# The third layer of a position-bias MLP on tiles of 32 keys by four sums, with lane transfers given out at fixed slots

## The chip, the cores and the metric

The kernel runs on one core of one Trainium2 chip. The time of a run is the device time of that core in microseconds (us). Everything is in float32.

## The reference, cut to what matters

The program has two layers on x of shape (2, 512, 32, 32). The first is a deformable attention with 8 heads of 64 channels: each head of each image looks from 1024 queries at 64 sampled keys, and the score gets a bias from a small MLP on the distance between query and key. The second is a plain attention over 1024 tokens. The change touches only the bias MLP:

```python
pos = grid_q[:, :, None, :] - grid_kv[:, None, :, :]     # 16 (image, head) groups, 1024 queries, 64 keys, 2
bias = jnp.sign(pos) * jnp.log1p(jnp.abs(pos))
bias = jax.nn.relu(bias @ cpb_w1 + cpb_b1)               # 2 -> 128
bias = jax.nn.relu(bias @ cpb_w2 + cpb_b2)               # 128 -> 128
bias = (bias @ cpb_w3 + cpb_b3).reshape(b, GROUPS, H * W, Hd * Wd)   # 128 -> 1
sim = jnp.einsum('bhid,bhjd->bhij', qh, kh) + bias
attn = jax.nn.softmax(sim, axis=-1)
out = jnp.einsum('bhij,bhjd->bhid', attn, vh)
```

There are 16 x 1024 x 64 pairs of query and key, and each needs the 128 x 128 product of the second layer.

## The kernel before, in words

**Slots.** The first stage works through `NS` = 256 slots, 16 for each of the 16 groups. A slot holds 4 keys by 1024 queries. In each, VectorE (DVE) builds the first layer `h1` (`st_layer1`, line L681, three buffers, two slots ahead). TensorE (PE) multiplies it by the second layer's weights (`st_layer2`, L698). The 128 hidden channels go out in four quarters z of 32, and four matmuls with 32 output columns each, one per key q, stand side by side in the PE array. So one eviction tile has on its 128 partitions 4 keys by 32 channels. ScalarE (ACT) evicts the four quarters with the relu: the even ones into `rx` (L707, three buffers), the odd ones into a long-lived tile and into `ub` (L709). PSUM has three tiles for this (`zp`, bufs=3).

**Sums over channels.** The third layer has one output, so its weights (`sc`) can be applied to whole tiles, and channels can be added before PE sees them. The channels are sorted by the sign of their third-layer weight, so that in quarters 1 and 3, which are evicted with the weight as a scale, lanes that are to be added share one sign. `st_sum(s, 0)` and `st_sum(s-1, 2)` are DVE instructions (L717) that add quarter 0 to quarter 1 and quarter 2 to quarter 3. Then an accumulating DMA on GpSimd's queue (POOL, L719) adds `ub` into the slot's long-lived tile. What is left of a slot is 4 keys by 32 sums.

**Folding lanes.** DMAs then fold the lanes (partitions) of a tile further. `st_fold` adds half of the lanes onto the other half, which frees half of the tile; `st_join` copies the partner tile's lanes into the freed half (SP queue, L743) and adds the partner's other lanes on top (POOL queue). Two slots so become one tile of 8 keys by 16 sums. `st_fold2` and `st_join2` (copies at L752) do the same with two such tiles: 16 keys by 8 sums. All adds go through `add` (L736), a POOL accumulate-DMA which is held behind the one before it in program order. The long-lived tile of slot s has the name `ua` (s%4 = 0, four buffers), `uc` (s%4 = 2, two) or `uo` (odd s, three). The tile `uc` becomes free when `st_join2` has read it.

**Third layer.** `st_layer3` (L784) multiplies such tiles by block weights (`w3f`) into the group's score tile in PSUM. For each 8 slots it issues one set of four matmuls with 32 columns each (two tiles by two halves of the queries), 12 slots after the first of the 8 slots. The product of queries and keys (L767) goes into the same PSUM tile. The last four slots of the last group aren't folded but multiplied tile by tile (`w3u`).

**Order.** The loop at the end of the stage writes out each slot by hand: the DVE sum of the slot before, the fold and join steps that are due, the next table load (`load_tables`, L650, a broadcast DMA `fb` on SP), `st_layer1(s+2)`, `st_layer2(s)`, tables, `st_sum(s, 0)`, then a step of background work (`later`, which makes the sampled keys and values of the next groups: `chain` and `sample`, with DMA loads `xn`, `xnt`, `wk` on SP), a step of the softmax of an earlier group (`softmax_steps`), and `st_layer3`. `st_join` follows its first slot by 3 slots, `st_fold2` by 4, `st_join2` by 6. Engines run their own instructions in this order; a DMA that waits holds up what is behind it on the queue of its engine.

After the stage come projection (`project`, L988), MLP (L1041, L160) and the second layer (L1200, L1276, L1298), which use the same product routines before and after the change.

Of the kernel before, what the change touches and what calls it, by code (L numbers as in the profile page):

```python
# [14 lines left out]
P = 128  # L15
# [42 lines left out]
def conv_seq_kernel(ctx: ExitStack, tc: tile.TileContext, x, xt, kst, pst, cst, vec, wsm, outw, w1, w2, wl, wlt, brow, out):  # L58
# [25 lines left out]
    w3f = cp.tile([P, 48], F32, name="w3f")  # L84
# [122 lines left out]
    with tc.tile_pool(name="lp", bufs=2) as lp:  # L207
# [11 lines left out]
        prod = ph.tile([P, 12, 2, 8, 8], F32, name="prod")  # L219
# [22 lines left out]
        nc.gpsimd.dma_start(out=pz[:, 0:413], in_=pst)  # L242
        nc.gpsimd.dma_start(out=ident, in_=kst)

        def load(b, k, wq=None):
# [21 lines left out]
        w2t, crow, tri, eight, chan, mask = (  # L267
            pz[:, a:b] for a, b in ((0, 128), (128, 256), (256, 384), (384, 392), (392, 393), (393, 413))
        )
        wb = vs[:, VOFF["w3"] : VOFF["w3"] + 2]  # L270
        po_, rn, t8, pc, dc, k8, one = (
            pw_[:, a:b] for a, b in ((0, 1), (1, 3), (3, 4), (4, 5), (5, 6), (8, 16), (128, 256))
# [15 lines left out]
        def order():  # L288
            nc.vector.tensor_scalar(k8, eight, rn[:, 1:2], 8.0, ALU.is_le, ALU.mult)
            nc.vector.tensor_reduce(t8, k8, AX.X, ALU.add)  # L290
            free, bound = ([t.rearrange("p (a b l) -> p b a l", a=2, b=2)[:, i] for t in (place, crow)] for i in (0, 1))
            nc.vector.tensor_scalar(bound[0], bound[1], t8, 64.0, ALU.is_ge, ALU.mult)
            nc.vector.tensor_tensor(bound[0], bound[0], bound[1], ALU.add)
            nc.vector.tensor_scalar(free[0], free[1], t8, None, ALU.add)
            nc.vector.tensor_scalar(perm, place, pc, None, ALU.is_equal)

        def arrange():
            nc.gpsimd.memset(prod, 0.0)
            ps = simp.tile([P, 512], F32, name="sim")
            nc.tensor.matmul(ps[:, 0:P], w2t, perm, start=True, stop=True)  # L300
            for z in range(4):
                for u in range(4):
                    nc.tensor.matmul(
                        ps[32 * u : 32 * u + 32, P + 2 * z : P + 2 * z + 2], perm[:, 32 * z : 32 * z + 32], wb,
                        start=True, stop=True,
                    )
            nc.scalar.copy(cw2, ps[:, 0:P])
            nc.scalar.copy(
                sc[:, 0:8].rearrange("p (a z) -> p z a", a=2), ps[:, P : P + 8].rearrange("p (z a) -> p z a", a=2)
            )  # L310
            nc.gpsimd.tensor_scalar(sc[:, 8:9], sc[:, 1:2], 0.0, 2.0, ALU.is_ge, ALU.mult)
            nc.gpsimd.tensor_scalar(sc[:, 8:9], sc[:, 8:9], 1.0, None, ALU.subtract)
            nc.gpsimd.tensor_scalar(sc[:, 0:4], sc[:, 0:4], sc[:, 8:9], None, ALU.mult)
            for z in (1, 3):
                nc.gpsimd.tensor_tensor(sc[:, 4 + z : 5 + z], sc[:, 4 + z : 5 + z], sc[:, z : z + 1], ALU.mult)
            nc.gpsimd.tensor_scalar(w3f[:, 16:32], mask[:, 0:16], sc[:, 8:9], None, ALU.mult)
            nc.gpsimd.tensor_scalar(w3u[:, 28:32], mask[:, 16:20], sc[:, 8:9], None, ALU.mult)
# [4 lines left out]
        def chain(ci):  # L322
# [52 lines left out]
            else:  # L375


                for m in range(3):
# [71 lines left out]
            fe = ph.tile([P, 5, n], F32, tag="fe", name="fe")  # L450
            pos, ab, u, ln, er = (fe[0:64, i, :] for i in range(5))
            nc.vector.tensor_scalar(pos, thf[0:64, 2 * n : 3 * n], -1.0, gq[0:64], ALU.mult, ALU.add)
# [8 lines left out]
            nc.vector.scalar_tensor_tensor(er, u, 1.0, ab, ALU.subtract, ALU.subtract)  # L461
            rc = acc.rearrange("p a k y x -> p (a k y x)")[0:64, 0:n]
            nc.vector.reciprocal(rc, u)
            nc.vector.tensor_tensor(er, er, rc, ALU.mult)
            nc.vector.tensor_scalar(pos, pos, 0.0, 2.0, ALU.is_ge, ALU.mult)
            yield
            nc.vector.tensor_tensor(ln, ln, er, ALU.subtract)
# [10 lines left out]
        def sample(ci):  # L478
# [10 lines left out]
            sg = ph.tile([P, 5, 2, K * J], F32, tag="fe", name="sg")  # L489
            hat = sg[:, 0:4].rearrange("p a f j -> p (a f j)")[:, 0 : 4 * K * J]  # L490
# [4 lines left out]
            nc.vector.tensor_tensor(sg[:, 4], sg[:, 0], sg[:, 1], ALU.mult)  # L495
            hx = ph.tile([P, 2, K, J], F32, tag="hx", name="hx")
# [5 lines left out]
            for i, (b, k) in enumerate(G):  # L502
                g = b * NCH + k
                xnt = ph.tile([P, 8, P], F32, name="xnt")
# [12 lines left out]
                kv, uv = (ph.tile([P, J], F32, name=name) for name in ("kv", "uv"))  # L517
                rowwise, natural = "p (e i t) -> p e i t", "p (i e t) -> p e i t"
                for f in range(2):
                    r, v = slice(64 * f, 64 * f + 64), sg[:, 4, f, i * J : (i + 1) * J]  # L520
                    nc.scalar.activation(
                        uv[r].rearrange(rowwise, e=2, t=16), v[r].rearrange(natural, e=2, t=16), AF.Copy,
                        scale=col("bn1b", k)[r],
                    )
# [6 lines left out]
                for t in range(8):  # L531
# [5 lines left out]
                nc.scalar.activation(  # L537
                    kv.rearrange(rowwise, e=2, t=16), ps[:, 0:J].rearrange(natural, e=2, t=16), AF.Copy,
                    scale=bns[:, k : k + 1],
                )  # L540
# [150 lines left out]
        def st_layer2(s):  # L691
            h1 = h1s.pop(s)
            r = []
            for z in range(4):
                ps = zp.tile([P, 2, 512], F32, name="ps2")
                for h in range(2):
                    for q in range(4):
                        nc.tensor.matmul(  # L698
                            ps[32 * q : 32 * q + 32, h, :], cw2[:, 32 * z : 32 * z + 32],
                            h1[:, 16 * h : 16 * h + 16, q, :], start=True, stop=True,  # L700
                        )
                name, bufs = (
                    ("rx", 3), (("ua", 4), ("uo", 3), ("uc", 2), ("uo", 3))[s % 4], ("rx", 3), ("ub", 3)
                )[z]
                o = lp.tile([P, 2, 512], F32, name=name, bufs=bufs)
                if z % 2 == 0:
                    nc.scalar.activation(o, ps, AF.Relu, bias=sc[:, 4 + z : 5 + z])  # L707
                else:
                    nc.scalar.activation(o, ps, AF.Relu, bias=sc[:, 4 + z : 5 + z], scale=sc[:, z : z + 1])  # L709
                r.append(o)  # L710
                if z % 2 == 1:
                    evicted.setdefault(s, []).append(nc.cur_bb.bb.instructions[-1])
# [28 lines left out]

        def st_join(s):
            nc.sync.dma_start(out=lanes(s, 1), in_=lanes(s + 1, 1))  # L743
# [6 lines left out]
        def st_join2(s):  # L750
            for o, i in zip(twos(s, 1), twos(s + 2, 1)):
                nc.sync.dma_start(out=o, in_=i)  # L752
            for o, i in zip(twos(s, 1), twos(s + 2, 0)):
                add(o, i)


        def st_layer3(s):
            gi, i = divmod(s // 8, NSL // 8)
            b, k, f = groups[gi]
            if gi not in sims:  # L760
                sims[gi] = simp.tile([P, 512], F32, name="sim")
            if f == 0 and i == 1:

                assert state[chain_of[b, k][0]] is None
                sims[gi + 1] = simp.tile([P, 512], F32, name="sim")
                for f_, h_, o, h in QUADS:
                    nc.tensor.matmul(  # L767
                        sims[gi + o][h_, :], kz[f_, b * NCH + k, :], qa[f_, b, k, h * 512 : (h + 1) * 512],
                        start=(o == 1), stop=False,
                    )  # L770
            w = w3f[:, 16 - 16 * i : 48 - 16 * i]
            parts = [[(w, sums[s + 4 * e][1])] for e in range(2)]
            if s + 8 == NS:

                w = [w3u[:, 28 - 16 * i - 4 * o : 60 - 16 * i - 4 * o] for o in range(4)]
                parts[1] = [(w[o], sums[s + 4 + o][1]) for o in range(4)]
                parts[1].append((w[3], sums[s + 7][3]))
                parts[0] = 4 * [None] + parts[0]
            for m in range(len(parts[1])):
                for h in range(2):  # L780
                    for e in range(2):
                        if parts[e][m]:
                            q, (w_, t) = 64 * h + 32 * e, parts[e][m]
                            nc.tensor.matmul(  # L784
                                sims[gi][q : q + 32, :], w_, t[:, h, :], start=(i == 0 and f == 0),
                                stop=(i == 1 and m == len(parts[e]) - 1),
                            )
            for o in range(8):
# [58 lines left out]
        for s in range(NS):  # L847
            if s > 0:
                st_sum(s - 1, 2)
            if s % 2 == 0 and 2 <= s < NS - 2:  # L850
                st_fold(s - 2)
            if s % 2 == 1 and 3 <= s < NS - 1:
                st_join(s - 3)
            if s % 4 == 0 and s >= 4:
                st_fold2(s - 4)
            if s % 4 == 2 and s >= 6:
                st_join2(s - 6)
# [15 lines left out]
            if bg is not None and state.get(len(CHAINS) - 1, 0) is None:  # L873
# [8 lines left out]
                opt = op.tile([P, 2, 512], F32, name="opt")  # L882
# [12 lines left out]
            if s % 8 == 4 and s >= 12:  # L895
                st_layer3(s - 12)
                if s % NSL == 4:
                    tails.append(softmax_steps(s // NSL - 1))
        st_sum(NS - 1, 2)
        st_layer3(NS - 8)  # L900
# [35 lines left out]
    with ExitStack() as top, tc.tile_pool(name="wp", bufs=1) as wp:  # L936
# [199 lines left out]
        project(0, op0[0], op0[1], opt, lambda: [next(tail, None) for _ in range(3)])  # L1136
# [313 lines left out]
def _order(np):  # L1450
# [4 lines left out]
    place = np.where(z % 2 == 1, 8 * (l // 4) + l % 4 + 4 * (z // 2), 32 * (z // 2) + l)  # L1455
    crow = np.broadcast_to(place, (P, P))
    tri = d[:, None] < d[None, :]
    eight = np.broadcast_to(8 * np.arange(1, 9), (P, 8))
    four = (4 * (d % 4) + d // 32)[:, None] == np.arange(16)
    alone = (d // 32)[:, None] == np.arange(4)  # L1460
    return np.concatenate([crow, tri, eight, d[:, None], four, alone], axis=1).astype(np.float32)
# [88 lines left out]
```

## Time and profile before

| what | value |
|---|---|
| three runs | 2617.99, 2619.43, 2620.34 us |
| profiled execution, its own time | 2621.32 us |
| its span | 2619.2 us |
| mean granted TensorE clock | 1.00 |
| PE busy in the span | 2603.2 us, 99% |
| DVE | 2313.1 us, 88% |
| ACT | 1750.3 us, 67% |
| POOL | 815.7 us, 31% |
| DMA packets' time on queue q0 (issued by POOL) | 54.6% of 16 engines |
| DMA packets' time on queue q1 (issued by SP) | 15.8% |

The profiled execution lasted 2.1 us longer than its span, and 1.9 us longer than the median of the runs. Busy times are sums over an engine's own instructions; two engines at once count twice. PE records a float32 matmul as two, so counts of matmul records are twice the program's. The first stage ends at about 1892 us of the span.

### The profile page before, as it was taken

How to read it: one execution, taken by the hardware profiler on the slowest of the kernel's cores; microseconds unless marked ns; L12 is line 12 of the kernel's file. 1: busy time of each engine (PE TensorE's matmuls, PEld its weight loads, DVE VectorE, ACT ScalarE, POOL GpSimd, SP SyncE). 2: the span in 40 equal slices, each digit the busy share in tenths (PEclk: the TensorE clock that was granted, in tenths of full speed). 3: DMA queues.
4: the chain of work that ended last, by engine and by line, in shares of the span. 5: the costliest groups of instructions: out<-in, count | busy, mean ns of one | idle time of the engine just before them, and what ended most of it. 6: DMA issues, size and time to landing. Idle time of an engine off the chain costs nothing.

```text
span 2619.2 us, 48156 instructions
## 1 busy us (share of the span) xinstructions
PE 2603.2 (99%) x19752; PEld 1019.5 (39%) x19752; DVE 2313.1 (88%) x1463; ACT 1750.3 (67%) x2325; POOL 815.7 (31%) x909
## 2 busy tenths in 40 slices
PE   9999999999999999999999999999999999999999
PEld 3333322333233232333333333334355665646556
DVE  7999999999999999999999999999776587666656
ACT  5887898878888887887887777777733242314041
POOL 1333333333333333333333333333332334200100
PEclk9999999999999999999999999999999999999999
DMA  5788877888887888787887888788787768400202
GB/s 188 176 174 185 190 171 168 182 182 195 169 178 171 180 171 200 173 179 166 185 182 165 180 177 177 167 185 177 151 211 169 150 143 172 91 17 1 73 0 57
DMA packets 167531, 407.74 MB, mean 156 GB/s; under 512 B 24944, under 2 KB 73216, under 8 KB 164624
## 3 DMA queue, kind: packets, MB, share of 16 engines
q0 software_dynamic: 100736, 259.43, 54.6%
q1 hardware_dynamic: 66144, 144.93, 15.8%
q8 instruction: 156, 2.56, 0.4%
q14 instruction: 63, 0.52, 0.1%
q10 hardware_dynamic: 432, 0.31, 0.0%
HBM read 82.15 MB, written 6.55 MB: 34 GB/s over the span
## 4 chain that ended last, share of the span: by engine, by line
PE 93%; DVE 3%; ACT 2%; issue 1%; DMA 0%; DVEq 0%; ACTq 0%
PE ps L698 64%; PE sw L1041 7%; PE sw L1200 7%; PE sw L160 6%; PE sw L988 2%; PE sw L1298 2%; PE sim L784 1%; PE psg L600 1%; DVE hm L137 1%; ACT rx L707 1%; PE psx L1276 1%; PE pkv L534 0%; PE sim L767 0%; PE pt L801 0%; PE pb L834 0%
## 5 line engine op out<-in xcount | busy, mean ns | idle before, releaser
L698 PE MATMUL ps<-h,cw 128*32 128x512 f32 x16384 | 1776.0, 592 | 6.1 <-ACT rx L707 5.0
L681 DVE CUSTOM_DVE_ANT_1 h<-ta,tb 128x4096 f32<-128x4096 f32 (+1 forms) x257 | 1130.5, 4399 | 29.6 <-PE ps L698 26.8
L698 PEld LDWEIGHTS ps<-h,cw 128*32 128x32 f32 x16384 | 538.0, 110 | 1209.1 <-issue 1144.6
L707 ACT ACTIVATE rx<-ps,sc 128x1024 f32<-128x1024 f32 x512 | 568.2, 1110 | 146.3 <-PE ps L698 125.7
L709 ACT ACTIVATE ub<-ps,sc 128x1024 f32<-128x1024 f32 x256 | 308.3, 1204 | 92.7 <-PE ps L698 92.6
L717 DVE SCALAR_TENSOR_TENSOR ub<-rx,sc,ub 128x1024 f32<-128x1024 f32 x256 | 326.3, 1275 | 6.6 <-ACT ub L709 6.6
L736 POOL DMA_DIRECT2D ua<-uc x126 | 154.8, 1241 | 301.6 <-DMA ua<-uc 291.7
L736 POOL DMA_DIRECT2D ua<-ua x189 | 219.0, 1319 | 28.8 <-DMA ua<-uo 22.3
L719 POOL DMA_DIRECT2D uo<-ub x127 | 124.4, 980 | 232.3 <-DVE ub L717 217.6
L1041 PE MATMUL sw<-hm,w2t 128*128 128x512 f32 x448 | 193.8, 592 | 0.2 <-DVE hm L125 0.2
L709 ACT ACTIVATE uo<-ps,sc 128x1024 f32<-128x1024 f32 x128 | 154.3, 1205 | 51.4 <-PE ps L698 51.0
L717 DVE SCALAR_TENSOR_TENSOR uo<-rx,sc,uo 128x1024 f32<-128x1024 f32 x128 | 163.3, 1276 | 8.1 <-ACT uo L709 8.1
L736 POOL DMA_DIRECT2D uc<-uo x63 | 53.1, 842 | 319.4 <-DMA uc<-uo 314.4
L1041 PEld LDWEIGHTS sw<-hm,w2t 128*128 128x128 f32 x448 | 85.0, 190 | 104.3 <-issue 99.0
L137 DVE TENSOR_TENSOR hm<-hm,sw 128x512 f32<-128x512 f32 (+1 forms) x80 | 58.7, 738 | 70.4 <-PE sw L160 50.6
L719 POOL DMA_DIRECT2D ua<-ub x64 | 58.9, 921 | 170.8 <-DVE ub L717 163.5
L661 ACT ACTIVATE ta<-fb,vs 128x512 f32<-128x512 f32 (+1 forms) x65 | 89.3, 1377 | 8.0 <-DMA fb<-fdr 8.0
L709 ACT ACTIVATE ua<-ps,sc 128x1024 f32<-128x1024 f32 x64 | 77.1, 1204 | 20.4 <-PE ps L698 20.1
L709 ACT ACTIVATE uc<-ps,sc 128x1024 f32<-128x1024 f32 x64 | 77.2, 1206 | 20.2 <-PE ps L698 17.1
L1364 POOL DMA_DIRECT2D xs<-rs x6 | 7.2, 1195 | 259.2 <-DVE rs L137 259.2
L166 ACT COPY hm<-sw 128x512 f32<-128x512 f32 x24 | 14.1, 586 | 110.1 <-PE sw L160 110.1
L717 DVE SCALAR_TENSOR_TENSOR uc<-rx,sc,uc 128x1024 f32<-128x1024 f32 x64 | 81.6, 1275 | 2.7 <-ACT uc L709 2.5
(294 smaller groups left out, 2657.7 us busy)
## 6 DMA issues: line engine op xcount, KB each, us to landing
uo<-ub POOLq DMA_DIRECT2D x127, 512.0 KB, 5.5
fb<-fdr SPq DMA_DIRECT2D x64, 512.0 KB, 5.2
ua<-ub POOLq DMA_DIRECT2D x64, 512.0 KB, 5.7
uc<-ub POOLq DMA_DIRECT2D x64, 512.0 KB, 5.1
ua<-ua POOLq DMA_DIRECT2D x63, 256.0 KB, 6.2
ua<-uo SPq DMA_DIRECT2D x63, 256.0 KB, 2.4
ua<-uo POOLq DMA_DIRECT2D x63, 256.0 KB, 5.8
uc<-uc POOLq DMA_DIRECT2D x63, 256.0 KB, 6.9
```

The lines of the kernel that those rows point to most:

```text
L137: nc.vector.tensor_tensor(out, a, b_, op)
L160: nc.tensor.matmul(bank[:, e, :], w, x, start=(q in (1, 2, 5) and e == k == 0), stop=True, skip_group_check=True,)
L661: nc.scalar.activation(ta.rearrange("p j x -> p x j")[:, :, j0:j1], fb[:, 0, :, j0:j1], AF.Identity, bias=col("cb1"), scale=col("w1x"),)
L681: nc.vector._custom_dve(TENSOR_ADD_SAT, out=h1[:, y : y + step].rearrange("p y t x -> p (y t x)"), in0=a.unsqueeze(1).to_broadcast([P, ste ...
L698: nc.tensor.matmul(ps[32 * q : 32 * q + 32, h, :], cw2[:, 32 * z : 32 * z + 32], h1[:, 16 * h : 16 * h + 16, q, :], start=True, stop=True,)
L707: nc.scalar.activation(o, ps, AF.Relu, bias=sc[:, 4 + z : 5 + z])
L709: nc.scalar.activation(o, ps, AF.Relu, bias=sc[:, 4 + z : 5 + z], scale=sc[:, z : z + 1])
L717: nc.vector.scalar_tensor_tensor(r[1], r[0], sc[:, z : z + 1], r[1], ALU.mult, ALU.add)
L719: nc.gpsimd.dma_start(out=sums[s][1], in_=sums[s][3], accum_op=ALU.add)
L736: nc.gpsimd.dma_start(out=out, in_=in_, accum_op=ALU.add)
L1041: nc.tensor.matmul(ps[:, m, :], w[:, a, k, m * P : (m + 1) * P], x[:, b_, k, :], start=(k == 0), stop=(k == 1),)
L1200: nc.tensor.matmul(ps[:, m, :], w[:, a, k, c + m * P : c + (m + 1) * P], x[b_][:, k, :], start=(k == 0), stop=(k == nk - 1),)
```

## The change

**A third level of folds.** For the first 13 groups (`FULL` = 208 slots) two tiles of 16 keys by 8 sums are folded once more into one of 32 keys by 4 sums: `st_fold3`, `st_copy3` and `st_join3`, each made of four DMAs of 64 KB. The third layer is then one set of four matmuls for a group's 16 slots. The last three groups keep tiles of 16 keys, with two sets each, and the last group keeps its four unfolded slots.

**Fixed delays.** Copies are split from the joins. A table (`LEVELS`, `LAST`) says how many slots after the first of its slots each transfer is given out; within one slot folds go ahead of copies and joins.

| transfer | before | after | last group after |
|---|---|---|---|
| fold | 2 | 2 | 2 |
| copy (SP) / join (POOL) | 3 / 3 | 3 / 4 | 3 / 3 |
| fold2 | 4 | 6 | 4 |
| copy2 / join2 | 6 / 6 | 7 / 8 | 6 / 6 |
| fold3 | - | 11 | - |
| copy3 / join3 | - | 14 / 15 | - |
| third layer | 12 after the first of 8 slots | 27 after the first of 16 slots (22 in the last three groups) | after the last slot |

**Buffers.** The tile of s%8 = 0 is now `u8` (four buffers), that of s%8 = 4 `u4` (two). To make room, the background work's scratch tiles share memory: `prod` lies in the memory of `xnt` and is cleared anew for each of the five chains but the first, where it was cleared once; `fe` and `sg` have three slices where they had five; `hx`, `kv` and `uv` lie in other tiles' memory; `opt` is allocated at its use. `order` has one DVE instruction fewer, because it now gives the 64 channels of quarters 1 and 3 one sign altogether, where it did so by blocks of eight; `pst` brings 24 more columns of constants.

```diff
+        def st_copy(s):
+            nc.sync.dma_start(out=lanes(s, 1), in_=lanes(s + 1, 1))
+
         def st_join(s):
-            nc.sync.dma_start(out=lanes(s, 1), in_=lanes(s + 1, 1))
             add(lanes(s, 1), lanes(s + 1, 0))
...
+        def fours(s, i):
+            t = sums[s][1].rearrange("(l a e) h n -> l a e (h n)", a=2, e=4)[:, i]
+            return [t[:, e] for e in range(4)]
+
+        def st_fold3(s):
+            for o, i in zip(fours(s, 0), fours(s, 1)):
+                add(o, i)
+
+        def st_copy3(s):
+            for o, i in zip(fours(s, 1), fours(s + 4, 1)):
+                nc.sync.dma_start(out=o, in_=i)
+
+        def st_join3(s):
+            for o, i in zip(fours(s, 1), fours(s + 4, 0)):
+                add(o, i)
+
+        FULL = NS - 3 * NSL
+        LEVELS = (
+            (8, FULL, (st_copy3, st_join3, st_fold3), (14, 15, 11)),
+            (4, NS - 4, (st_copy2, st_join2, st_fold2), (7, 8, 6)),
+            (2, NS - 4, (st_copy, st_join, st_fold), (3, 4, 2)),
+        )
+        LAST = {st_copy2: 6, st_join2: 6, st_fold2: 4, st_join: 3}
...
-            w = w3f[:, 16 - 16 * i : 48 - 16 * i]
-            parts = [[(w, sums[s + 4 * e][1])] for e in range(2)]
-            if s + 8 == NS:
+            if s < FULL:
+                parts = [[(w3f[:, 0:32], sums[s + 8 * i][1])] for i in range(2)]
+            else:
+                w = [w3f[:, 48 - 16 * e : 80 - 16 * e] for e in range(2)]
+                parts = [[(w[e], sums[s + 8 * i + 4 * e][1]) for e in range(2)] for i in range(2)]
+            if s + NSL == NS:
...
-                    ("rx", 3), (("ua", 4), ("uo", 3), ("uc", 2), ("uo", 3))[s % 4], ("rx", 3), ("ub", 3)
+                    ("rx", 3), (("u8", 4), ("uo", 3), ("uc", 2), ("uo", 3), ("u4", 2), ("uo", 3), ("uc", 2), ("uo", 3))[s % 8],
+                    ("rx", 3), ("ub", 3),
...
-            if s % 2 == 0 and 2 <= s < NS - 2:
-                st_fold(s - 2)
-            if s % 2 == 1 and 3 <= s < NS - 1:
-                st_join(s - 3)
-            if s % 4 == 0 and s >= 4:
-                st_fold2(s - 4)
-            if s % 4 == 2 and s >= 6:
-                st_join2(s - 6)
+            for _, move, a in sorted(due.get(s, ()), key=lambda e: e[0]):
+                move(a)
...
-            if s % 8 == 4 and s >= 12:
-                st_layer3(s - 12)
-                if s % NSL == 4:
-                    tails.append(softmax_steps(s // NSL - 1))
+            for t in (27, 22):
+                if s % NSL == t % NSL and s >= t and (s - t < FULL) == (t == 27):
+                    st_layer3(s - t)
+                    tails.append(softmax_steps((s - t) // NSL))
         st_sum(NS - 1, 2)
-        st_layer3(NS - 8)
+        st_layer3(NS - NSL)
...
+                prod = ph.tile([P, 12, 2, 8, 8], F32, tag="xnt", name="prod")
+                nc.gpsimd.memset(prod, 0.0)
...
-            nc.vector.tensor_scalar(k8, eight, rn[:, 1:2], 8.0, ALU.is_le, ALU.mult)
-            nc.vector.tensor_reduce(t8, k8, AX.X, ALU.add)
+            nc.vector.tensor_scalar(t8, rn[:, 1:2], 64.0, 64.0, ALU.is_ge, ALU.mult)
```

## The prediction

> **What bounds the kernel now.** I read the table of busy time by engine, then the chain that ended last, then stretches of the first stage, then the two queues behind PE: POOL's waits and the DMA traffic.
>
> ```profile
> PE 2603.2 (99%) x19752; PEld 1019.5 (39%) x19752; DVE 2313.1 (88%) x1463; ACT 1750.3 (67%) x2325; POOL 815.7 (31%) x909
> PE 93%; DVE 3%; ACT 2%; issue 1%; DMA 0%; DVEq 0%; ACTq 0%
> 38.00:1892.00 1854.00, 1847.81 (x17284) 577.00 (x17278) 1806.45 (x908) 1516.29 (x1971) 651.66 (x760) 1.00 0.82 176
> 400.00:500.00 100.00, 97.96 (x912) 29.31 (x908) 100.00 (x60) 84.19 (x116) 33.60 (x40) 1.00 0.81 172
> L698 PE MATMUL ps<-h,cw 128*32 128x512 f32 x16384 | 1776.0, 592 | 6.1 <-ACT rx L707 5.0
> ```
>
> The third row is the first stage; its columns are the stretch, then busy time (and count) of PE, weight load, DVE, ACT and POOL, the clock, the DMA share and GB/s. PE is busy for 1847.8 of 1854.0 us and makes 93% of the chain, and its second layer lost only 6.1 us to waits. So PE time taken out of this stage shortens it, until another engine is next. That is near: DVE has 1806.5 of 1854.0 us, 47.5 us of air, and the fourth row is a stretch in which DVE, with background work, was never idle and PE was busy for 97.96 of 100 us.
>
> ```profile
> 890.84 41.20 PE ps L698 x384
> 949.11 0.86 PE sim L784 x8
> 1028.65 6.72 DMA xn<-in_x
> 1423.61 1.21 ACT L709 ACTIVATE ub<-ps,sc 128x1024 f32<-128x1024 f32 x1 [0.60 <-PE ps L698]
> 1427.05 1.21 ACT L709 ACTIVATE uc<-ps,sc 128x1024 f32<-128x1024 f32 x1 [0.60 <-PE ps L698]
> 1429.70 1.28 DVE L717 SCALAR_TENSOR_TENSOR ub<-rx,sc,ub 128x1024 f32<-128x1024 f32 x1
> 1431.28 0.88 POOL L719 DMA_DIRECT2D uo<-ub  x1 [2.15 <-DVE ub L717]
> ```
>
> The first three lines are pieces of the chain (start, duration): six slots of second layer in 41.20 us, so 6.87 us a slot (64 matmul records); one third-layer set of eight records, 0.86 us; a late load. The rest is the timeline of one slot: eviction, last DVE sum, and the transfer that adds `ub`.
>
> ```profile
> POOL uc L736 <- DMA uc<-uo: 314.4, 61, 9.4
> POOL ua L736 <- DMA ua<-uc: 291.7, 55, 7.7
> q0 software_dynamic: 56242, 189.71, 67.5%
> q1 hardware_dynamic: 27616, 74.89, 14.4%
> ua<-uc POOLq DMA_DIRECT2D x104, 128.0 KB, 5.6
> ```
>
> The first two are POOL's longest waits in the stage (total us, times, longest): a join stood behind its copy. The other three are from the DMA view of 200 to 1700 us: packets, MB and share of 16 engines for each queue, then an accumulate's median from issue to landing.
>
> [...] eight records of 592 ns each take 0.86 us. Hence I price a set at 0.86 us and not at 8 x 0.592 = 4.7 us. [...] the shares of both queues, 67.5% and 14.4%, make up the 0.82 of the stage. So I add up the traffic of SP and POOL, and splitting copies from joins frees POOL's queue only, no DMA time.
>
> **The change part by part.**
>
> *PE.* Before, the third layer takes 31 sets and 5 in the last step, 36. After, 13 (one for each full group), 2 x 2 for groups 13 and 14, and 6 in the last: 23. Saved: 13 x 0.86 = 11.2 us. Query-key products, second layer and transposes are the same in number. The last step has one set more than before (0.86 us, already in the 23).
>
> *DVE.* One small instruction less in `order`, nothing else. By starts, a slot of `st_layer1` and two sums takes 4.33 + 1.20 + 1.20 = 6.73 us of DVE, against 6.87 on PE. The stage shrinks to 1843 us with DVE at 1806: 36 us of air stay, but thinly spread. `h1` is ready 5 to 11 us ahead of PE in most slots (1.9 us at the least), so the 0.86 us that PE gains once in 16 slots is covered. Where background work makes DVE the last for a while, as at 400 us, the gain is not had in that stretch: some 1 us lost in all.
>
> *POOL and DMA.* fold3 and join3 add 26 x 8 = 208 POOL DMAs of 64 KB and copy3 26 x 4 = 104 on SP. POOL's queue: the trace shows 0.8 to 1.8 us for an issue and about 0.55 us pitch back to back; POOL is busy for 652 of 1854 us, so 208 x 1.2 = 250 us more fit, and its long waits behind copies shrink, since a join now follows its copy by a slot. DMA engines: q0 costs 67.5% x 1500 / 189.71 = 5.34 us a MB, q1 14.4% x 1500 / 74.89 = 2.88. Added are 13.6 MB of accumulates (73 us) and 6.8 MB of copies (20 us): 93 us over the 1500 us of the first 13 groups, so the share goes from 0.82 to 0.88. Hidden while nobody waits for a landing.
>
> *Who waits for landings.* After: copy at 3, join at 4, fold2 at 6, copy2 at 7, join2 at 8, fold3 at 11, copy3 at 14, join3 at 15 slots, the third layer at 27. join3 of the second half is at 23, four slots (27 us) ahead of PE against a landing of 5.6. So PE's own wait goes on being nothing. The eviction buffers are tighter. `uc` (two buffers, one per four slots) of slot s = a+2 is last read by join2(a), which moves from slot a+6 to a+8; slot a+10 evicts into it. From the end of the `ub` eviction at 1424.82 (1423.61 + 1.21) to a `uc` eviction two slots later it is 2 x 6.87 + 1427.05 - 1424.82 = 15.97 us. Needed are 6.16 to the end of the DVE sum (1430.98), 0.30 to the issue of the `ub` add, about 1.1 until both adds of join2 are issued behind it, and 5.6 to land: 13.2 us. The margin is 2.8 us, where it was 2.8 + 13.7. Three PSUM tiles cover about 2 us more. In lags (DVE's last sum comes up to 6 us later around slots 46 to 66, 112 to 116 and 166 to 172, when background work stands in front) the margin is gone: ACT waits for `uc`, PE for PSUM. Each such slot costs PE 0 to 4 us, but the lag is also let off by it. There are some 6 such reuses: bounds 0 and 12 us, I take 2, since only what the lag exceeds of 2.8 + 2 is lost and DVE catches up meanwhile.
>
> *Background scratch.* `prod` cleared four times on POOL, 4 to 7 slots before use: nothing. The `xn` load of chain 2 moves behind copy3s on SP, that of chain 4 no longer stands behind a late copy2; before, that wait shows in the chain (6.72 us) and cost PE 2.5 us. Between +2.5 and -2.5; I take -1. `opt` and the rest: nothing, at the same place as before.
>
> *The end.* Group 14's softmax starts two slots later than before (22 after its first slot, where it was 20), so about two more steps are left over: 1 to 2 us of ACT beside projection's matmuls; I take 0.5.
>
> Sum, against the profiled execution's 2621.3: -11.2 + 1 + 2 - 1 + 0.5 = -8.7, so 2612.6. The median of the runs is 1.9 lower than the profiled execution: 2610.7, say 2610.
>
> **The rivals.** *A: the gain is mostly given back.* DVE is next: its 36 us of air are not where PE gains, and the lags cost the upper bound of 12 us less what is hidden. For it: the row at 400 us and DVE at 97% of the stage. Against it: the lead of `h1`. A loss of 6 to 12 us in place of 2.5 gives 2613 to 2621, centre 2616.
>
> *B: slower, by late lane transfers.* The mechanism is the `uc` reuse above. At a DMA share of 0.88 accumulates land later than 5.6 us: the slowest in the trace took 10.8, which makes the margin 2.8 - 5.2 = -2.4. It decides once the usual landing passes 5.6 + 2.8 + 2 = 10.4 us in ordinary slots: then about half of the 52 reuses in the first 13 groups would lose about 1 us each, up to all of them; 26 to 40 us lost less 11 gained is +15 to +29, but lags would be self-limiting, so +6 to +26: 2625 to 2645, centre 2632. For it: even slots now carry 1280 KB of accumulates where 1024 were, 1.31 MB x 5.34 = 7.0 us in a slot of 6.87, so queues build up over a slot and drain in the odd one. Against it: 0.12 of the engines' time stays free, and a burst of half a slot is not a standing queue.
>
> *C: the change doesn't do what it says.* The counts exclude it: w3f matmuls fall from 126 to 74 in the program.
>
> **How the numbers follow.** The main case has 0.58 (own range 2606 to 2614, from losses of 0 to 6 us), A 0.22, B 0.20. About 0.2% (5.2 us) is what a measurement of this kernel can tell from no change. Faster is below 2614.2: nearly all of the main case and 0.04 of A make 0.61. Same is 0.18 of A and a bit of the others: 0.20. Slower is B: 0.19. The range takes in the main case, A, and the mild start of B: 2604 (gain with the `xn` wait gone and nothing lost: 2619.4 - 11.2 - 2.5 = 2605.7, less 1.7 for the spread of runs) to 2627.
>
> **What would show it.** Third-layer records on PE: 148 with `w3f` where 252 were. PE's busy time in the stage down by 11 us, with the idle time before the second layer still below 10 us. DMA share of the stage near 0.87. POOL's waits for its copies down from 606 us to below 300. If B is right, waits of ACT's evictions for DMAs into `uc` or `ub` appear, and second-layer waits for ACT grow to tens of us. If A is right, second-layer waits for DVE's `h` or for ACT grow by 6 to 12 us near background work. What would make me wrong: landings of accumulates far above 6 us at a share of 0.88, or SP's queue holding up the table load `fb` behind a waiting copy3.

## The result, and the profile after

The changed kernel took 2639.45 us (median of 4 runs, 2636.25 to 2642.91) against 2619.4 us before: a ratio of 1.0077, 95% interval 1.006 to 1.0095. It is slower by 20 us, where 2610 was forecast and 2604 to 2627 was the range. The profiled execution took 2642.9 us with a span of 2641.1.

First the page of the changed kernel: busy time by engine, the chain by engine, the second layer's group; and two stretches (columns as in the prediction; the first is the stage, whose second layer now ends at 1898 us and not at 1892).

```profile
PE 2600.4 (98%) x19648; PEld 1003.7 (38%) x19648; DVE 2310.4 (87%) x1462; ACT 1746.5 (66%) x2324; POOL 980.5 (37%) x1121
PE 62%; DMA 11%; issue 10%; DVE 10%; POOL 5%; ACT 2%; SPq 0%; DVEq 0%; POOLq 0%; ACTq 0%
L693 PE MATMUL ps<-h,cw 128*32 128x512 f32 x16384 | 1777.8, 593 | 18.0 <-ACT rx L703 11.8
...
38.00:1898.00 1860.00, 1841.87 (x17172) 560.75 (x17160) 1804.29 (x907) 1512.20 (x1969) 816.21 (x968) 1.00 0.88 186
1900.00:1920.00 20.00, 9.47 (x38) 3.01 (x39) 2.48 (x2) 1.57 (x5) 5.69 (x6) 0.74 0.37 79
```

PE has 104 matmul records less, 13 sets of eight (`w3f` 148 where 252 were), as the change says. But PE idles: 18.0 us ahead of the second layer where it was 6.1, and the chain now runs through DMA, DVE and POOL as well. The last row is the new thing: in the 20 us at the end of the stage PE is busy for 9.5, at a granted clock of 0.74. The waits of PE in the first stage say where (total us, times, longest):

```profile
PE ps L693 <- ACT rx L703: 11.8, 13, 4.4
PE sim L815 <- DMA u<-uc: 11.1, 1, 11.1
PE ps L693 <- ACT uc L705: 3.2, 1, 3.2
PE ps L693 <- DVE h L676: 1.6, 2, 0.8
PE ps L693 <- ACT ub L705: 0.7, 2, 0.4
```

To see where time is lost I took, in each trace, the start of the first second-layer record of every slot (64 records each), counted from slot 0, and subtracted the same of the kernel before. The next column is the end of the last second-layer record, the last the time from there to the end of the span (profiled executions, us; minus is ahead of before):

| kernel | slot 32 | 48 | 64 | 112 | 128 | 224 | stage | rest |
|---|---|---|---|---|---|---|---|---|
| changed | -1.4 | +4.3 | +4.8 | +2.0 | +3.7 | -1.0 | +6.3 | +15.7 |
| e4, no third-level transfers | -1.4 | -2.0 | -1.3 | -4.1 | -5.6 | -10.5 | -3.3 | +15.2 |
| e6, the same cut to 1/8 bytes | -1.4 | -1.1 | -0.6 | -3.5 | -4.4 | -9.1 | -2.0 | +16.8 |
| e8, delays alone | +0.3 | +1.5 | +2.0 | +1.6 | +1.3 | +1.2 | +1.6 | +1.2 |
| e1, folded tile last | -1.4 | +2.6 | +3.0 | +0.2 | -0.2 | -4.9 | +2.3 | +11.2 |
| e2, 15 groups on 32 keys | -1.2 | +6.4 | +7.0 | +4.1 | +2.7 | -2.1 | -3.0 | +13.0 |
| e13, short delays in last 8 slots | -1.3 | +4.4 | +5.0 | +2.2 | +2.1 | -2.6 | +4.7 | +5.1 |
| e3, e1 with e2 | -1.4 | +1.0 | +1.5 | -1.3 | +0.1 | -4.6 | -5.5 | +15.4 |
| e5, e3 with e13 | -1.3 | +3.4 | +3.9 | +1.1 | +2.7 | -2.0 | -2.9 | +4.1 |
| e7, e5 with table loads in odd slots | -1.3 | +2.8 | +3.4 | +0.6 | -0.9 | -5.5 | -6.4 | +3.1 |
| e9, e7 with `xn` a slot later | -1.4 | -2.5 | +4.6 | +1.7 | +1.5 | -3.7 | -4.6 | +3.1 |
| e12, best version | -1.3 | +0.6 | +1.1 | -1.7 | -0.4 | -5.1 | -6.1 | +1.3 |

Up to slot 218 six of these kernels issue the same instructions: changed, e1, e2, e13, e3 and e5. Yet they stand at +1.0 to +6.4 at slot 48 and at -1.0 to -4.9 at slot 224. A few us between two rows in these columns are therefore no difference. The way from slot 224 to the end of the stage repeats (+7.3, +7.2 and +7.3 in changed, e1 and e13). The trace of the changed kernel is also the slowest of its four runs.

In the changed kernel three stretches lose: slots 32 to 48 and around 118 (ordinary slots), 224 to the end of the stage (+7.3), and what follows the last second layer (+15.7).

**The end.** The timeline of the changed kernel around the last third-layer step:

```profile
1893.82 0.48 SPq L739 DMA_DIRECT2D uc<-uo  x1
1894.39 9.61 SPq L750 DMA_DIRECT2D u<-uc  x2
1900.25 0.83 POOL L732 DMA_DIRECT2D uc<-uo  x1 [7.17 <-DMA u<-uc]
1907.78 0.81 POOL L732 DMA_DIRECT2D u<-uc  x1 [4.96 <-DMA u<-uc]
1910.53 1.92 PE L815 MATMUL sim<-u,w3f 128*32 128x512 f32 x4 [11.09 <-DMA u<-uc]
```

and that of the kernel before:

```profile
1888.27 0.81 POOL L736 DMA_DIRECT2D ua<-uc  x1 [5.17 <-DMA ua<-uc]
1892.05 1.03 PE L784 MATMUL sim<-ua,w3u 128*32 128x512 f32 x4
```

The last join2 (slots 248 to 251) was issued at 1888.27, ahead of the end of the second layer at 1892.2; it is now issued at 1907.78, 9.4 us behind that end (1898.4). And the new code multiplies this tile first of six, where it was the fifth step: nothing is left to do meanwhile.

**The evictions of slots 228 and 244.** Groups 13 and 14 keep tiles of 16 keys, so their `u4` tiles (slots 212 and 220) are held until the third layer at slot 230. There are two `u4` buffers, and slot 228 needs the first:

```profile
1713.88 1.92 PE L815 MATMUL sim<-u,w3f 128*32 128x512 f32 x16
1715.86 1.21 ACT L705 ACTIVATE u<-ps,sc 128x1024 f32<-128x1024 f32 x1 [0.74 <-PE sim L815]
1717.10 1.28 DVE L713 SCALAR_TENSOR_TENSOR u<-rx,sc,u 128x1024 f32<-128x1024 f32 x1 [1.14 <-ACT u L705]
```

The eviction of slot 228's quarter 1 (the trace leaves buffer numbers out) stands behind the third layer of slot 230, two slots late. A PSUM tile is held meanwhile, DVE's sum and POOL's add follow late, and the lead of `h1` falls from 9 us to 0.15 us at slot 232. Slots 244 to 248 show the same.

### The profile page after: what moved, and what is told of

It is laid out like the page before. It is cut to its first block, busy times and chain, and to the rows that moved or that the text cites. A ratio compares the mean times of both kernels' runs of the same rounds, so it can differ in the third digit from the quotient of the medians.

```text
span 2641.1 us, 48908 instructions
## 1 busy us (share of the span) xinstructions
PE 2600.4 (98%) x19648; PEld 1003.7 (38%) x19648; DVE 2310.4 (87%) x1462; ACT 1746.5 (66%) x2324; POOL 980.5 (37%) x1121
## 4 chain that ended last, share of the span: by engine, by line
PE 62%; DMA 11%; issue 10%; DVE 10%; POOL 5%; ACT 2%; SPq 0%; DVEq 0%; POOLq 0%; ACTq 0%
PE ps L693 37%; PE sw L1065 7%; PE sw L1226 7%; PE sw L160 6%; DMA u<-uc 4%; DVE h L676 3%; POOL u L732 3%; DVE ub L713 2%; DMA uc<-uc 2%; PE sw L1324 2%; PE psg L595 1%; DMA uc<-uo 1%; DMA u<-u 1%; PE sim L815 1%; DMA w1e<-w1e 1%
## 5 line engine op out<-in xcount | busy, mean ns | idle before, releaser
L693 PEld LDWEIGHTS ps<-h,cw 128*32 128x32 f32 x16384 | 525.8, 110 | 1238.6 <-issue 1138.5
L732 POOL DMA_DIRECT2D u<-u x397 | 402.6, 1488 | 16.2 <-DMA u<-ub 6.4
L713 DVE SCALAR_TENSOR_TENSOR ub<-rx,sc,ub 128x1024 f32<-128x1024 f32 x256 | 326.6, 1276 | 10.5 <-ACT ub L705 10.5
L715 POOL DMA_DIRECT2D uo<-ub x127 | 113.8, 896 | 583.1 <-DVE ub L713 535.7
L732 POOL DMA_DIRECT2D u<-uc x126 | 125.1, 1255 | 35.1 <-DMA u<-uc 34.1
L715 POOL DMA_DIRECT2D uc<-ub x64 | 58.4, 912 | 188.0 <-DVE ub L713 147.5
L715 POOL DMA_DIRECT2D u<-ub x64 | 56.3, 880 | 168.3 <-DVE ub L713 166.8
L732 POOL DMA_DIRECT2D uc<-uc x63 | 107.2, 1701 | 0.0
L732 POOL DMA_DIRECT2D uc<-uo x63 | 92.9, 1475 | 35.3 <-DMA uc<-uo 20.6
L732 POOL DMA_DIRECT2D u<-uo x63 | 85.9, 1364 | 24.1 <-DMA u<-uo 20.7
```

The source lines that it names most:

```text
L693: nc.tensor.matmul(ps[32 * q : 32 * q + 32, h, :], cw2[:, 32 * z : 32 * z + 32], h1[:, 16 * h : 16 * h + 16, q, :], start=True, stop=True,)
L713: nc.vector.scalar_tensor_tensor(r[1], r[0], sc[:, z : z + 1], r[1], ALU.mult, ALU.add)
L715: nc.gpsimd.dma_start(out=sums[s][1], in_=sums[s][3], accum_op=ALU.add)
L732: nc.gpsimd.dma_start(out=out, in_=in_, accum_op=ALU.add)
```

## The experiments

### The order of the last step, and 15 groups on 32 keys (e1, e2, e3)

```diff
-                parts[1][1:] = [(w[o], sums[s + 12 + o][1]) for o in range(4)] + [(w[3], sums[s + 15][3])]
+                last = parts[1][0]
+                parts[1] = [(w[o], sums[s + 12 + o][1]) for o in range(4)] + [(w[3], sums[s + 15][3]), last]
```

```diff
-        FULL = NS - 3 * NSL
+        FULL = NS - NSL
```

> The changed kernel, with one edit: in the last third-layer step the folded tile of slots 248 to 251 is multiplied last, behind the four unfolded slots, where the changed kernel multiplies it first. Theory 1 (separate places: the order of the last step, the u4 buffers of the last groups, and late landings in ordinary slots) expects PE to work some 4 to 6 us of matmuls inside the 11.1 us wait, and the wait to be 5 to 7 us at the end of the step: 4 to 6 us faster than the changed kernel, about 2634. Theory 2 (all lateness is DMA load) expects the same here, since the transfers land when they land. If the step's order were the whole cause of the end's loss, the time would fall by 11 to 15 us to about 2626.

> The changed kernel with 15 groups on tiles of 32 keys in place of 13 (FULL = NS - NSL), so that no tile of the u4 name is held until a third-layer step except in the last group. That adds 4 folds, 4 copies and 4 joins of the third level per group and so DMA load. Theory 1 expects the two evictions that waited for the third layer (slots 228 and 244) to wait no more, the transfers of the last group to be on time, and 2 sets less: 6.5 + 1.7 + some 8 to 12 us at the end, so 2619 to 2624. Theory 2 (load) expects no gain or a loss beyond the 1.7 us of two sets: 2637 to 2642.

> Both edits: 15 groups on tiles of 32 keys, and the folded tile of slots 248 to 251 last in the last step. Theory 1 expects the end to be as in the kernel before, and only the 10 to 11 us lost in ordinary slots to remain against the 11 to 13 us of PE time saved: 2616 to 2620. Theory 2 expects 2632 or more.

Measured: 2634.30 us for the order (ratio 1.0057, 1.0042 to 1.0072), 2632.64 for 15 groups (1.0049, 1.0034 to 1.0064), 2631.98 for both (1.0044, 1.0029 to 1.0059). The order gave the 5 us that were expected; PE still waited 6.6 us in the step. With 15 groups the stretch from slot 224 to the end of the stage, +7.3 us against before in the changed kernel, is at -0.9 (-2.1 to -3.0): 1.7 us of the 8.2 are for two sets, the rest for the evictions, which no longer wait. But the end hardly moved: 15 groups missed theory 1's 2619 to 2624, and both edits together missed its 2616 to 2620 by 12 us. PE's wait in the last step of the run with both edits:

```profile
PE sim L816 <- DMA uc<-ub: 10.0, 1, 10.0
```

It is for the add of slot 254, behind the late joins on POOL's queue. So the queue itself was late, for a reason that theory 1 lacked.

### Bytes or issues of the third level, and the delays alone (e4, e6, e8)

```diff
-            (8, FULL, (st_copy3, st_join3, st_fold3), (14, 15, 11)),
```

```diff
-            return [t[:, e] for e in range(4)]
+            return [t[:, e, 0:128] for e in range(4)]
```

The third is the kernel before with the `LEVELS` lines for folds of 2 and 4 slots, and the third layer at `s % 8 == 6`, 14 slots behind.

> The changed kernel without the third level's transfers (no fold3, copy3, join3), all else as it is: third layer once a group for 13 groups, same delays and buffers. It leaves out part of the sum over channels, so the scores lack it. It takes the added 93 us of DMA time away and leaves the later join2 (8 slots) in place. If the losses in ordinary slots (10 to 11 us up to slot 208) come from DMA load, they fall to the 7 us of waits of the kernel before: 8 to 11 us faster than the changed kernel, 2629 to 2631. If they come from the shorter time between the last read of a uc tile and its reuse alone, the time stays at 2637 to 2640. The u4 tiles of the last groups and the order of the last step are not touched, so their losses stay in both cases.

> The changed kernel with every third-level transfer cut to the first 128 of 1024 elements of a lane: as many DMAs on the queues of POOL and SP as in the changed kernel, an eighth of their bytes. It leaves out part of the third-level sum, so the scores lack it. Without those transfers the losses in ordinary slots were gone (10.5 us ahead of the kernel before at slot 224). If it was their bytes on the DMA engines, the same shows here: 2631 to 2634, 9 to 11 us ahead at slot 224. If it was the 208 and 104 issues on the two queues, the losses stay: 2637 to 2641, about even with the kernel before at slot 224.

> The kernel before, with the fixed delays alone: copies split from joins (3 and 4, 7 and 8, fold2 at 6, the short ones in the last 8 slots), third layer at 14 slots instead of 12, still two sets a group, no third level, and the buffers and scratch of before. If the delays and the later join2 cost nothing by themselves, it stays within 3 us of the kernel before, 2616 to 2622. If the shorter time to the reuse of uc costs by itself, it is slower by more than 5 us.

Measured: 2632.31 us without the transfers (1.0049, 1.0032 to 1.0066), 2635.53 with an eighth of their bytes (1.0059, 1.0042 to 1.0075), 2622.94 for the delays alone (1.0013, 1.0006 to 1.0019). Queue shares from 200 to 1700 us of the changed kernel (first two lines) and without the transfers (last two):

```profile
q0 software_dynamic: 62598, 202.91, 74.1%
q1 hardware_dynamic: 30786, 81.42, 16.4%
```

```profile
q0 software_dynamic: 56570, 190.85, 68.2%
q1 hardware_dynamic: 27616, 74.89, 14.5%
```

Without the transfers the saving on PE is had nearly in full: 10.5 us ahead at slot 224, where 14 sets less are some 12 us. e4 keeps the shared scratch tiles, so they cost little in ordinary slots. With all the issues but an eighth of the bytes it is 9.1 us. Both lie clear of the six kernels with whole transfers (1.0 to 4.9 us ahead), so the losses in ordinary slots come with these transfers, and mostly with their bytes. The 1.4 us between e4 and e6 are within the spread, so what the issues cost isn't shown. One place still lost time in e6: at slot 118 PE waited 1.9 us for ACT's eviction into `uc`, in e4 not at all. In time e4 took 7.1 us off the changed kernel and e6 3.9; both came out above what was expected if the bytes were the cause (2629 to 2631, 2631 to 2634). The later join2 stayed in both, so it isn't the cause alone. The delays alone cost 3.4 us, between the two branches expected. Neither run touched the end, whose loss stayed.

### The last group's delays (e5, e13)

```diff
-                    t = times[kind] if a < NS - NSL else LAST.get(moves[kind], times[kind])
+                    t = times[kind] if a < NS - NSL // 2 else LAST.get(moves[kind], times[kind])
```

> The kernel of the run with both edits (15 groups on 32 keys, folded tile last), with the short delays kept for the last 8 slots in place of the last 16. In that run POOL's queue was 1 to 1.7 slots late in the last group, because joins there again stand on the queue behind their copies while group 14's third-level transfers are still due; PE waited 10.0 us in the last step for the add of slot 254. If that is the cause of what is left at the end, the wait falls to 0 to 4 us and the clock is not lowered by it: 8 to 14 us faster, 2618 to 2624. If the last transfers are late for the DMA load alone, nothing changes: 2629 to 2634.

> The changed kernel with one edit: the short delays kept for the last 8 slots only instead of the last 16. If POOL's queue in the last group is late because of the short delays there by themselves, most of the 11.1 us wait in the last step and the lowered clock behind it go: 9 to 14 us faster than the changed kernel, 2626 to 2630. If the two evictions that wait for the third layer (slots 228 and 244) make the queue late too, the wait stays above 5 us and the gain is 2 to 6 us.

Measured: 2619.54 us on top of both edits (ratio 1.0, 0.9992 to 1.0009), 2628.91 as the only edit of the changed kernel (1.0032, 1.0023 to 1.0041). By itself it took 10.5 us off, and 12.4 us off the run with both edits. PE's wait in the last step with it alone, and on top of both:

```profile
PE sim L815 <- issue: 2.4, 1, 2.4
```

```profile
PE sim L816 <- DMA uc<-ub: 1.7, 1, 1.7
```

That shows what made the end late: the short delays over 16 slots. With them copy and join are given out in the same slot, and POOL's queue stands behind the copy: in the timeline above it was idle for 7.17 us ahead of the add of 1900.25 and for 4.96 us ahead of the join2 of 1907.78. What is behind on the queue waits too: slot 254's sum on DVE ended at 1895.04 us (1893.76 + 1.28), and its add was issued at 1901.32, behind two others. From slot 249 on the chain of the changed kernel runs through such transfers, one behind the other, up to the third layer (three of its pieces: start, duration):

```profile
1858.27 3.22 DMA u<-uo
1903.53 3.72 DMA u<-uc
1907.78 2.50 DMA u<-uc
```

With 8 such slots the queue nearly keeps up, even with the held evictions of slots 228 and 244 still there: in e13 the last join2 is issued 0.7 us behind the end of the second layer. Why 16 are too many isn't shown. The kernel before has the short delays in every slot, and its last join2 came in time. That the transfers of group 14, still due with their longer delays, put the queue behind fits the timeline, but no run tested it.

### Mending the ordinary slots (e7, e9, e10, e11, e12)

Waits of ACT up to the end of the stage in the changed kernel, then its wait for an `xn` load in the kernel before:

```profile
ACT xn L328 <- DMA xn<-in_x: 6.0, 1, 6.0
ACT uc L705 <- DMA uc<-uc: 6.0, 4, 4.2
ACT uc L705 <- DMA u<-uc: 5.0, 4, 1.5
```

```profile
ACT xn L330 <- DMA xn<-in_x: 2.7, 1, 2.7
```

The two `xn` waits are for different loads. That of before is for chain 4's, at 1035 us; it is gone after. The 6.0 us are for chain 2's load. It was issued at 307.6 us in both, and landed and was used at 316.5 before, without a wait, and at 320.3 after: not issued later, but landing later. In the five other kernels with the same instructions it landed at 318.3 to 321.7, in e4 at 313.1.

Slot 118 in the changed kernel (the first line is a piece of the chain):

```profile
895.41 10.59 DMA u<-uc
906.15 1.21 ACT L705 ACTIVATE uc<-ps,sc 128x1024 f32<-128x1024 f32 x1 [4.19 <-DMA uc<-uc]
907.41 5.07 PE L693 MATMUL ps<-h,cw 128*32 128x512 f32 x32 [3.15 <-ACT uc L705]
```

The profile names `uc<-uc` for ACT's wait, but the last DMA that landed ahead of the eviction is the add out of `uc`, join2's, at 906.00.

The edits on e5: table loads in slots with s%4 = 1 where their chain is done (e7); on top of that a `yield` more between the load and its use in chain 2 (e9), or third-level copies and joins at 15 and 17 slots (e10), or both, with slot 254's tile last in the last step (e11); at last e9 with the `yield` behind that use taken out in exchange, and slot 254's tile last (e12):

```diff
                 if i == 0:
                     xn, wq = xn0.pop()
+                elif ci == 2:
+                    yield
                 nc.scalar.activation(xn, xn, AF.Identity, bias=col("bn1b", k), scale=bns[:, k : k + 1])
-                if ci > 0:
+                if ci > 0 and (ci, i) != (2, 1):
                     yield
...
+                parts[1] = [(w[o], sums[s + 12 + o][1]) for o in (0, 1, 3)]
+                parts[1] += [last, (w[3], sums[s + 15][3]), (w[2], sums[s + 14][1])]
...
-            if s % 4 == 0 and s // 4 + 1 < 4 * NG:
-                load_tables(s // 4 + 1)
+            c = (s + 3) // 4 + 1
+            if s % 4 in (0, 1) and (s == 0 or s > 1) and c < 4 * NG and c not in raw and c not in tabs and (
+                s % 4 == 0 or chain_of[groups[c // 4][0:2]] [0] in state
+            ):
+                load_tables(c)
```

> The kernel with short delays in the last 8 slots only, and the table loads given out three slots earlier, in slots with s%4 = 1, where fewer lane transfers are due, wherever their chain is done by then. If bursts in the slots with s%4 = 0 (join, join2, fold, z-add and a table load together) make the loads of xn and the joins late, the losses in ordinary slots (some 10 us) fall by 2 to 6 us against the run without this. If only the mean load counts, no difference beyond 2 us.

> The run with the table loads in odd slots, with one background slot more between the second xn load of chain 2 and its use. There ACT waited 4.5 us for that load, PE 3.1 us for ACT, and PE's matmuls after it were recorded at twice their pitch for some 3 us. If the late load is the cause of that loss, it goes: 4 to 6 us faster than that run, and the difference to the kernel before at slot 48 falls from +2.8 to about -2. If something else at that place (POOL, uc) held PE, the wait turns up one slot later and nothing is gained.

> The run with the table loads in odd slots, with the third level's copies at 15 and joins at 17 slots instead of 14 and 15, so that both are given out in odd slots, where fewer accumulates are due; the bytes are the same. If the losses are of bursts, ACT's waits for DMAs into uc (5.8 us there) and the stall at slot 118 fall to near nothing: 2 to 4 us faster than that run. If they are of the mean load (0.92 of the DMA engines from 200 to 1700 us), no difference.

> Both of these edits, and in the last step the tile of slot 254, whose add lands last, multiplied last. Theory: the three losses in ordinary slots and the 1.9 us wait at the end are gone or small, and most of the 13 us of PE time that 15 sets less save is had: 2608 to 2613, faster than the kernel before. If the load on the DMA engines moves the wait elsewhere, 2615 to 2620.

> The run with the table loads in odd slots, with the xn load of chain 2 given a slot more as before, but its product given out in the same background step as its use, so that the rest of the chain keeps its slots (with the extra slot alone, the table load of slot 61 came 5.2 us late and PE lost 4.3 us there instead). In the last step the tile of slot 254 comes last; third-level delays are 14 and 15 again. If late loads are what is left of the loss before slot 64, the difference to the kernel before at slot 64 is -1 to -3 us where it was +3.4, and the time is 2611 to 2616, faster than the kernel before. If the lost time moves to a third place again, it stays at 2617 to 2621.

| run | us | ratio to before, 95% |
|---|---|---|
| e7 | 2620.25 | 1.0, 0.9992 to 1.0009 |
| e9 | 2618.42 | 0.9996, 0.9988 to 1.0004 |
| e10 | 2619.59 | 0.9997, 0.9989 to 1.0006 |
| e11 | 2618.55 | 0.9998, 0.999 to 1.0006 |
| e12 | 2614.84 | 0.9982, 0.9975 to 0.9988 |

Only e12 came into the time that its first theory gave; the four others missed it. The table loads in odd slots brought nothing that can be told (2620.25 against 2619.54). Other slots for the third level's transfers brought nothing either, and in e11 a join at 17 was late for the third layer at 27. In e9 the `xn` wait was gone (-2.5 at slot 48, where e7 had +2.8), but the chain was a slot later and the table load that needs it came late; at slot 64 nothing was won (+4.6). ACT's wait in e9, and PE's in e11 for a join3:

```profile
ACT ta L658 <- DMA fb<-fdr: 5.2, 1, 5.2
```

```profile
PE sim L819 <- DMA u<-u: 2.7, 1, 2.7
```

Only e12, which gave the load a slot without moving the chain, was clearly faster: 2614.84 us, 3.6 to 5.4 us below the other four and 4.9 us below the kernel before. ACT no longer waited for the load, which had cost it 4.3 to 7.4 us in the eight kernels with whole transfers and without the slot. A part of the gain is the order of the last step: PE's wait for slot 254's add, 1.9 us in e7, is gone. The +1.1 at slot 64 missed the -1 to -3 expected, and tells little (e3 had +1.5 without the slot). The longest of PE's waits in its stage:

```profile
PE ps L695 <- ACT rx L705: 4.8, 10, 1.7
PE ps L695 <- ACT uc L707: 2.5, 1, 2.5
PE ps L695 <- ACT ub L707: 0.7, 2, 0.4
```

The reuse of `uc` at slot 118 is still there. A third `uc` buffer would test it; no run did.

## Why the prediction was wrong, point by point

- **PE's saving: right.** 104 records less. PE's busy time in the stage fell only from 1847.8 to 1841.9 us, in part because two stretches of lowered clock (0.58 over 4 us each, with PE busy for 4.00 and 3.59 of them, so by estimate 1.7 and 1.5 us lost) count as busy there. e4, where PE waited for 1.9 us at the longest ahead of the second layer, had 10.5 us at slot 224.
- **DMA load: right, its cost mis-sized.** 0.88 of the stage was forecast and measured. I then held it hidden "while nobody waits for a landing". Medians to landing rose from 5.6 to 6.9 us for the adds out of `uc`, and from 5.2 to 6.8 for table loads, and that was enough for the tight places: e4 and e6 show that the ordinary slots lost time with these bytes.
- **`uc` reuse: the mechanism right, the size about right.** I took 2 us of a range of 0 to 12. ACT waited 11.0 us for DMAs into or out of `uc`; PE lost 3.2 us of it at one place, slot 118: the two adds of join2 were issued at 894.89 and 895.41, landed at 905.65 and 906.00, and the eviction into `uc` began at 906.15. Rival B's losses at half or all of the 52 reuses did not come. Its sign and its range (2625 to 2645) came true by other mechanisms, which is luck.
- **`xn` loads: a wrong sign.** I argued from its place in SP's queue and took -1. Chain 2's load was issued at the same time, landed 3.8 us later, and cost PE 4.5 us of waiting and, by the clock of 0.58 over the 4 us behind it, some 1.7 more. Chain 4's wait did come off, as foreseen, but it was worth less than the 2.5 us taken: 2.7 us were ACT's wait, and PE idled there for 1.1 and 0.25 us.
- **"PE's own wait goes on being nothing": the step that failed.** I counted join3 of an ordinary group against its third layer at 27 slots, and never did this for the last group, whose slack is the time to the end of the stage, nor for the order of its six sets; I costed the last step at one set more, and the end at 0.5 us. Measured: 11.1 us of wait for the last join2, some 1.7 us of lowered clock behind it (0.52, with PE busy for 3.47 us), and the rest, as far as is known, softmax and the set; 15.7 in all. e13 won back 10.6 of it.
- **Buffers of the last groups: left out.** The prediction names no reuse of `u4`. In full groups the tile is free 15 slots after the first of its 8 slots and wanted at 20. Slot 212's, in group 13, is free at slot 230 and wanted at 228; slot 228's likewise at 246 and 244. That is the 7.3 us from slot 224 on, and e2 won it back.
- **POOL's waits for copies: right.** From 679 us (314.4 + 291.7 + 72.5) to some 93 (34.1 + 25.1 + 20.6 + 13.4). POOL had no part in the chain before (PE 93%, DVE 3%, ACT 2%, issue 1%), and the fall paid for nothing.
- **Rival A** had the DVE row as its reason. PE's waits for `h` are 1.6 us; DVE was not the bound.

Sum against the forecast's 2610: 15 us at the end, 7 in the last groups' evictions and some 8 in ordinary slots more than I had make 30; measured are 29.5. The 8 us are of one trace; the six kernels with the same instructions give 4 to 8.

## What to carry to other kernels

When work per item is made deeper and later, check each special case for itself: the buffers' lifetimes in groups that take the old path, and what the last group still has to do when the main engine runs out of work. Give the piece that lands last the last place in the final sum. Traffic that fits in the mean is paid for where a load or a buffer reuse has the least slack, so list these places before calling it hidden (here chain 2's `xn` load, which landed 3.8 us later, and `uc` at slot 118, which cost PE 3.2 us); and mend one without moving its neighbours.

## What the runs showed of the hardware

Behind three of PE's waits in the changed kernel the granted clock was lower, so that they cost more than themselves; behind two shorter waits, in other runs, it was lower once and full once. Stretches of 4 us, of the changed kernel: behind its wait of 4.45 us at slot 38, the 4 us after that, behind the 11.1 us wait at the end and behind the 3.15 us wait at slot 118. Then one of e12, behind a wait of 2.5 us, and one of e13, behind a wait of 2.4:

```profile
322.60:326.60 4.00, 4.00 (x24) 0.80 (x24) 2.19 (x2) 2.95 (x3) 1.71 (x2) 0.58 1.00 188
326.60:330.60 4.00, 4.00 (x44) 1.11 (x40) 4.00 (x2) 3.59 (x6) 0.00 (x0) 0.99 0.61 182
1910.00:1914.00 4.00, 3.47 (x11) 0.96 (x14) 0.00 (x0) 0.00 (x0) 0.00 (x0) 0.52 0.02 4
907.00:911.00 4.00, 3.59 (x20) 0.91 (x24) 4.00 (x3) 4.00 (x11) 2.54 (x3) 0.58 0.75 157
902.50:906.50 4.00, 3.52 (x24) 1.00 (x28) 4.00 (x4) 4.00 (x11) 2.45 (x3) 0.69 0.72 167
1899.60:1903.60 4.00, 3.58 (x25) 1.38 (x28) 0.00 (x0) 0.00 (x0) 0.00 (x0) 1.00 0.01 4
```

The third figure from the end is the clock: 0.52 to 0.58 behind the first three waits (24 records in the first row, 44 in the next, at a clock of 0.99), but 0.69 and 1.00 behind two waits of nearly one length. PE's busy time in a row, times what the clock lacks to 1.00, is an estimate of what was lost on top of the wait: 1.7 us behind the waits of 4.45 and of 11.1 us, 1.5 behind that of 3.15, 1.1 in e12 and nothing in e13. Why the clock differs between these last two isn't shown.
